# A graph-attention and expert kernel on one core: the last two graphs' router sums taken by columns of row 0, their attention sums put into the products' banks, and the stored lower rows read as they lie

## The chip, the cores and the metric

The kernel runs on one core of a Trainium2 chip. A core has TensorE (PE, the matrix engine; the loads of its stationary operand are shown apart, as PEld), VectorE (DVE), ScalarE (ACT), GpSimd (POOL) and SyncE (SP, which here only issues transfers), an on-chip memory of 128 partitions, and eight accumulator banks of 128 x 512 f32 that only PE writes. The metric is the time on the device, in microseconds (us), median of several runs.

## What is computed

`x` holds 128 graphs of 128 nodes with 1024 features, `adj` one 128 x 128 matrix of zeros and ones for each. For every graph:

```python
x = x + gnn(layernorm(x), adj)      # Wh = x W; one attention weight for each source node and head
x = x + ffn(layernorm(x))           # ffn(y) = y + sum over 2 of 8 experts: up_e (down_e y) * gate_e
```

The gates of a graph come from row 0 of its normalized features alone: eight logits (row 0 times the router's eight rows), the two largest, and a softmax over them. `down` takes 1024 features to 16 for each expert (128 lower rows for all eight), `up` takes them back.

## The kernel before

Graphs are taken in pairs (q = 0 to 63), and pairs in groups of four graphs. A pair's projection `x W` is done with fewer products than the plain block scheme (seven per pair, of which some are shared with the neighbouring pair: the lines 561 and 640). Its result, split in a high and a low part (`parts`, made by `high` on ACT, L708, and by `low` on DVE, L712), is multiplied by the adjacency matrix (`attend`, L770); the attention weight, ELU and residual follow on DVE and ACT, then the second layer norm's sums, the transposed copy `y_t` that the experts read, the logits, the choice, and the expert products.

The order of the work is written out by hand: FIRST, EVEN, ODD and LAST are lists of short names. A name stands for a closure in a table (`does`), and each engine's instructions stand in the order in which the names call for them. Nothing reorders them: an instruction that waits holds up everything behind it on its engine. LAST is the list of the last step. A trailing `-` or `+` means the step before or the one after; the names with `+` come from `at_the_end()`, which treats the last group by itself:

- Set A is graphs 0 and 1 of that group, set C its graphs 2 and 3 (the last two of all; r = 0 and 1). Unlike all groups before, whose chosen experts' rows are fetched one slot at a time, these take all 128 lower rows and all 128 upper rows. `LW` (`load_all`) loads them over the weights that are no longer needed: `up_all`, and `down_of_rows`, in which a partition holds, for each of the 128 lower rows, eight consecutive values (k = 0 to 7, the eight blocks of 128 features).
- `OA` (`order_all`, L1037) copies `down_of_rows` on ACT so that for each k the 128 lower rows' values lie side by side (`down_all`).
- `dA`, `d0C`, `d1C` (`down_of`, L1210) are the lower products: for each k one matmul with 128 x 128 of `down_all` as the stationary operand, over 256 columns of `y_t` for set A (both graphs at once), over 128 columns for each graph of C.
- `A`, `w`, `E`, `a`, `b` + r + h: the attention sum of graph r, half h (L1054), its weighting into `sums_of` (L1060), the exponential (L1068), and the two parts of ELU added to `x` (L1072, L1079). `T` and `k`: transposing a half on PE (L1106) and copying it into `y_t` (L1109). `n`, `q`, `s`: the mean, the squares (L1088), the statistics on POOL.
- `PA`, `P0`, `P10`, `P11`: row 0 times the router's rows, elementwise (L1128, L1135); `R` sums, `L` and `V` (L1151, L1156) add over the partitions on PE; `ch`, `sp`, `rt`, `wg` choose and make the gates, `g` (L1219) multiplies the lower products by them. For set C row 0 is read from the transposed `x`, so the logits of C come after `T`.
- `u` + t + h + set (`up_of`, L1224): the upper product of one graph and half. `m` and `v`: its scaling on ACT (L1237) and its sum with `x` on POOL (L1247), or both at once on DVE (`add_of_up`, L1230). `m..B`, `v..B` finish the group before in the same way. Each half of `x` is stored as soon as it is complete.

Banks: `pw0` and `pw1` (two banks each) hold projections, `ph`, `pl`, `pd_all`, `pu` take turns in two more pairs (`double`, `single`). A name that needs a bank waits until its last reader is done.

Of the kernel before, what the change touches and what calls it, by code (L numbers as in the profile page):

```python
# [8 lines left out]
F32 = mybir.dt.float32  # L9
# [5 lines left out]
ALU = mybir.AluOpType  # L15
# [31 lines left out]
LAST = """  # L47
Jt2- n0- hi0- lo0- J7- J1- q0- ps3- Jt3- Jp- y1- ro1- Jr- I1- n1- t0- J2- Jd- sr- q1- ps2-
J5- It0- J4- st1- Ja- Js- st0- M7b- J3- It1- M7a- Ip- rj0- Je- rp- c22- I6- ss- L- It2- ch0-
hi3- I7- t1- ch1- It3- fr- M4a- fe4- M4b- jn1- Ir- fe0- c21- lo3- hi2- fe5- Ia- I4- ra- rs-  # L50
fe2- I5- fe1- I2- fe7- Is- I3- lo2- A1 Ie- fe6- Id- hi1- fe3- aw M1b lo1- M1a jn0- pe LW+
aw2 fe8- p1 A0 h1 M2a x1 M2b h0 rj1- x0 e1 eo y1 hi0 sc0 e0 lo0 y0 M6b M6a wg n1 q1 D t0 u2
u4 f n0 hi1 dn aw0+ lo1 M7a M7b LR+ q0 pe0+ c22 U0 M4b ss t1 hi3 M4a dw0+ v00 rj0 v01 rdA+
U1 m1B+ lo3 v1B+ m0B+ c21 aw1+ rj1 A00+ pe1+ hi2 A01+ w00+ w01+ v0B+ A11+ a01+ dw1+ a00+
E01+ jn1 b01+ m2B+ PA+ w11+ lo2 RA+ E00+ T01+ A10+ m3B+ b00+ w10+ n0+ LA+ OA+ a11+ a10+ q0+
s0+ E11+ VA+ T00+ dA+ E10+ chA+ k00+ b10+ spA+ b11+ k01+ T10+ T11+ n1+ v3B+ rtA+ wgA+ P11+
k11+ P10+ gA+ u00A+ q1+ P0+ m00A+ RC+ v2B+ LC+ u01A+ jn0 s1+ rdC+ chC+ VC+ m01A+ v00A+ v01A+
k10+ d1C+ spC+ rtC+ ac u10A+ d0C+ m10A+ wgC+ gC+ u11A+ j1+ u00C+ m11A+ u10C+ j0+ v10A+ u01C+
v10C+ v00C+ u11C+ v11C+ v01C+ v11A+
""".split()  # L60
# [3 lines left out]
def adj_ffn_kernel(  # L64
# [959 lines left out]
    down_of_rows = block[0][:, D:2 * D].rearrange("p (e r k) -> p e r k", e=E, r=R)  # L1024
    down_all = block[1][:, 0:D].rearrange("p (k e r) -> p k e r", e=E, r=R)
    router_all = block[1][:, D:D + E * KC]

# [5 lines left out]
    def load_router():  # L1033
        nc.sync.dma_start(router_all, router_table)

    def order_all():
        nc.scalar.copy(down_all, down_of_rows.rearrange("p e r k -> p k e r"))  # L1037

    def at_the_end():
# [10 lines left out]
        def attend_half(r, h):  # L1050
            if i + r not in PH:
                PH[i + r] = double("ph")
            for s in range(2):
                nc.tensor.matmul(PH[i + r][:, h], GRP[g]["adj_f"][:, 2 + r, :],  # L1054
                                 PARTS[p][:, s, NH * r + h], start=(s == 0), stop=(s == 1))
# [44 lines left out]
        def turn_half(r, h):  # L1100
            if h not in turned:
                turned[h] = slot_of(h)
            pt = turned[h][:, r].rearrange("p (c n) -> p c n", c=CPH)
            for c in range(CPH):
                k = h * CPH + c
                nc.tensor.transpose(pt[:, c], X[i + r][:, k * P:(k + 1) * P], ident)  # L1106

        def keep_half(r, h):
            nc.scalar.copy(y_of(i + r)[:, h * CPH:(h + 1) * CPH],  # L1109
                           turned[h][:, r].rearrange("p (c n) -> p c n", c=CPH))  # L1110

# [18 lines left out]

        def parts_of_half(r, h):
            k = slice(h * CPH, (h + 1) * CPH)
            part = prod_of("C")[:, r:r + 1, :, k]
            rows = turned[h][:, r].rearrange("p (o c n) -> p o n c", o=1, c=CPH)[:, :, 0:1]
            nc.vector.tensor_tensor(part, rows.to_broadcast(part.shape),  # L1135
                                    router[:, :, :, k].to_broadcast(part.shape), ALU.mult)

# [10 lines left out]
        def logits_of(s):  # L1148
            n = sets[s][1]
            got["pl", s] = double("pl")  # L1150
            nc.tensor.matmul(got["pl", s][:, 0, 0:n * E], ones, add_of(s)[:, 0:n * E], start=True,  # L1151
                             stop=True)

        def dev_of(s):
            n = sets[s][1]
            nc.tensor.matmul(got["pl", s][:, 1, 0:n], ones, add_of(s)[:, n * E:], start=True,  # L1156
                             stop=True)

        def choose_of(s):
            n = sets[s][1]  # L1160
            shape = [P, n, E]
            by_order = order[:, None].to_broadcast(shape)
            lg = got["pl", s][:, 0, 0:n * E].rearrange("p (g e) -> p g e", g=n)
            top = small.tile([P, TOP, n], F32, tag="top", name="top", bufs=2)
            val = got["val", s] = small.tile([P, 2, n, TOP], F32, tag="val", name="val", bufs=2)
            mark = small.tile(shape, F32, tag="mark", name="mark", bufs=2)
            for c in range(TOP):
                if c:
                    left = small.tile(shape, F32, tag="lg", name="lg", bufs=1)
                    nc.vector.tensor_tensor(mark, by_order, val[:, 0, :, 0:1].to_broadcast(shape),  # L1170
                                            ALU.is_equal)
                    nc.vector.scalar_tensor_tensor(left, mark, NO_ENTRY, lg, op0=ALU.mult,
                                                   op1=ALU.add)
                    lg = left
                nc.vector.tensor_reduce(top[:, c], lg, AX.X, ALU.max)
                nc.vector.tensor_tensor(mark, lg, top[:, c, :, None].to_broadcast(shape),
                                        ALU.is_equal)
                nc.vector.tensor_tensor(mark, mark, by_order, ALU.mult)
                nc.vector.tensor_reduce(val[:, 0, :, c], mark, AX.X, ALU.max)
            pr = got["pr", s] = small.tile([P, 2, n], F32, tag="pr", name="pr", bufs=2)  # L1180
            nc.vector.tensor_tensor(pr[:, 0], top[:, 1], top[:, 0], ALU.subtract)

        def spread_of(s):
            pr = got["pr", s]
            nc.vector.tensor_tensor(pr[:, 0], pr[:, 0], got["pl", s][:, 1, 0:sets[s][1]], ALU.mult)

# [5 lines left out]
        def gates_of(s):  # L1192
# [4 lines left out]
            nc.vector.tensor_mul(gate[:, :, 1], pr[:, 1], gate[:, :, 0])  # L1197
            val = val.rearrange("p v g s -> p v (g s)")
            hit = small.tile([P, n * TOP], F32, tag="own", name="hit", bufs=2)
            nc.vector.tensor_scalar(hit, val[:, 0], own_order, None, op0=ALU.is_equal)  # L1200
            nc.vector.tensor_tensor(hit, hit, val[:, 1], ALU.mult)
            gates = got["gate", s] = small.tile([P, n], F32, tag="gate" + s, name="gate_all", bufs=1)
            nc.vector.tensor_reduce(gates, hit.rearrange("p (g s) -> p g s", g=n), AX.X, ALU.add)

        def down_of(s, t, n):
            if ("pd", s) not in got:
                got["pd", s] = double("pd_all")[:, 0]
            first = sets[s][0] + t
            for k in range(KC):
                nc.tensor.matmul(got["pd", s][:, t * P:(t + n) * P],  # L1210
                                 down_all[:, k].rearrange("p e r -> p (e r)"),
                                 st["y_t"][:, k, first * P:(first + n) * P],
                                 start=(k == 0), stop=(k == KC - 1))

        def gate_of(s):
            n = sets[s][1]
            dn = got["dn", s] = work.tile([P, n, P], F32, tag=sets[s][3], name="dn_all", bufs=1)
            pd = got["pd", s][:, 0:n * P].rearrange("p (t n) -> p t n", t=n)
            nc.vector.tensor_tensor(dn, pd, got["gate", s][:, :, None].to_broadcast(pd.shape),  # L1219
# [40 lines left out]
        for t in range(G):  # L1260
            does.update({f"m{t}B": (scale_before, t), f"v{t}B": (add_before, t)})
        for t in range(2):
            for h in range(2):
                does.update({f"m{t}{h}A": (scale_up, "A", t, h)})
        for r in range(2):
# [3 lines left out]
                f"q{r}": (squares_at_end, r), f"s{r}": (stats_at_end, r), f"j{r}": (join, i + r),  # L1269
                f"d{r}C": (down_of, "C", r, 1)})  # L1270
            for h in range(2):
# [3 lines left out]
                    f"b{r}{h}": (below_half, r, h), f"T{r}{h}": (turn_half, r, h),  # L1275
                    f"k{r}{h}": (keep_half, r, h), f"P{r}{h}": (parts_of_half, r, h)})
        for s in sets:
# [4 lines left out]
            for t in range(2):  # L1282
                for h in range(2):
                    does.update({f"u{t}{h}{s}": (up_of, s, t, h), f"v{t}{h}{s}": (add_of_scaled if s == "A" else add_of_up, s, t, h)})
        does.update({"PA": (parts_of, "A", 0, 2, slice(0, KC)), "dA": (down_of, "A", 0, 2),
                     "P0": (parts_of, "C", 0, 1, slice(0, KC)), "LW": (load_all,), "LR": (load_router,),
                     "OA": (order_all,)})
        return does

# [181 lines left out]
```

## Time and profile before

| | us |
|---|---|
| median of three runs (1859.14 to 1860.34) | 1860.15 |
| the profiled execution, its own time | 1858.17 |
| its span, first to last instruction | 1856.3 |
| PE busy in the span | 1839.1 (99%) |
| DVE busy | 1578.4 (85%) |
| ACT busy | 1242.8 (67%) |
| last product of the projection (L561) ends | 1819.08 |
| last matmul ends | 1850.74 |

An engine's busy time is the union of its instructions. PE is pipelined: records of matmuls overlap, an f32 matmul leaves two records and two loads of its stationary operand, and the distance from one start to the next says more than the length of a record. The span ends some 4 us after the last addition, when the last stores have landed and the engines have met.

### The profile page before, as it was taken

To read this page: it belongs to the slowest core of one execution; us is meant where nothing else is said; L and a number is where in the kernel's file an instruction comes from. 1 tells how busy PE (TensorE), PEld (TensorE's weight loads), DVE (VectorE), ACT (ScalarE), POOL (GpSimd) and SP (SyncE) were. 2 spreads that over 40 slices of the span, in tenths; PEclk is the share of its full clock that TensorE was granted. 3 is DMA by queue.
4 is the path that set the end of the run, shared out by engine and by line. 5 is a ranking of instruction groups with operands and counts; after the bars stand their busy time and mean duration, and the time that the engine had idled before them with its cause. 6 is when DMAs were issued, how large, how long until landed. Compare 5 with 4: busy or idle time off the path is not lost.

```text
span 1856.3 us, 29668 instructions
## 1 busy us (share of the span) xinstructions
PE 1839.1 (99%) x10196; PEld 1504.2 (81%) x10196; DVE 1578.4 (85%) x3411; ACT 1242.8 (67%) x1423; POOL 1172.0 (63%) x1691
## 2 busy tenths in 40 slices
PE   9999999999999999999999999999999999999997
PEld 6888888888888888888888888888888888888884
DVE  6888888888888888888888888888888888888886
ACT  3666666766666766666666667666667676666676
POOL 4666656667566667566666566675666675666663
PEclk9999999999999999999999999999999999999998
DMA  8555566565576655666555665555665556665543
GB/s 321 151 175 140 186 199 177 185 180 149 183 197 190 182 152 168 192 184 194 177 138 187 199 177 183 179 150 183 194 194 182 136 184 192 184 193 173 136 160 114
DMA packets 349100, 330.42 MB, mean 178 GB/s; under 512 B 279196, under 2 KB 281372, under 8 KB 348440
## 3 DMA queue, kind: packets, MB, share of 16 engines
q1 hardware_dynamic: 331512, 287.09, 51.0%
q0 software_dynamic: 17008, 40.91, 7.4%
q8 instruction: 81, 1.33, 0.3%
q14 instruction: 67, 0.55, 0.1%
q10 hardware_dynamic: 432, 0.53, 0.1%
HBM read 194.24 MB, written 68.17 MB: 141 GB/s over the span
## 4 chain that ended last, share of the span: by engine, by line
PE 93%; POOL 3%; DVE 2%; issue 1%; ACT 0%; DMA 0%; DVEq 0%; POOLq 0%
PE pw L561 58%; PE pw L640 17%; PE ph L770 6%; PE pu L1006 4%; PE pd L986 3%; PE ix L640 3%; POOL down L971 2%; PE pd_all L1210 0%; POOL xt L493 0%; PE pu L1224 0%; ACT ph L802 0%; DVE w_sb L1293 0%; DVE w_sb L306 0%; POOL s L493 0%; PE idle L238 0%
## 5 line engine op out<-in xcount | busy, mean ns | idle before, releaser
L561 PE MATMUL pw<-w_sb,xt 128*128 128x260 f32 (+1 forms) x4080 | 959.3, 386 | 0.5 <-POOL w_sb L357 0.5
L561 PEld LDWEIGHTS pw<-w_sb,xt 128*128 128x128 f32 x4080 | 763.1, 190 | 169.2 <-issue 30.6
L971 POOL DMA_INDIRECT down<-table,at_down x248 | 249.3, 1005 | 197.2 <-DVE of_slot L935 116.1
L708 ACT ACTIVATE parts<-wh,rstd 128x512 fp32r<-128x512 f32 x192 | 135.2, 720 | 344.1 <-DVE wh L568 303.7
L849 ACT COPY y_t<-tt 128x2048 uint16<-128x2048 uint16 x126 | 314.6, 2497 | 1.3 <-DMA tt<-halves 1.3
L561 PE MATMUL pw<-w_sb,s 128*128 128x260 f32 (+1 forms) x1088 | 249.8, 382 | 0.0
L843 ACT COPY halves<-xn 128x2048 uint16<-128x2048 uint16 x126 | 237.5, 1885 | 2.5 <-DVE xn L793 2.0
L561 PEld LDWEIGHTS pw<-w_sb,s 128*128 128x128 f32 x1088 | 206.4, 190 | 34.1 <-DVE wh L568 0.9
L493 POOL TENSOR_TENSOR s<-xt 128x512 f32<-128x512 f32 x64 | 83.3, 1302 | 234.6 <-DMA xt<-in_x_t 234.6
L786 ACT ACTIVATE ph<-ph 128x1024 f32<-128x1024 f32 x126 | 127.9, 1015 | 80.4 <-DVE xn L783 73.6
L1015 DVE SCALAR_TENSOR_TENSOR xn<-pu,rstd,xn 128x512 f32<-128x512 f32 x244 | 168.7, 743 | 11.1 <-PE pu L1006 11.1
L776 DVE TENSOR_TENSOR ph<-ph,att 128x1024 f32<-128x1024 f32 x126 | 149.1, 1228 | 11.1 <-PE ph L770 4.5
L432 DVE BATCH_NORM_STATS2 stats<-xn 128x6 f32<-128x512 f32 x248 | 158.4, 680 | 0.0
L855 ACT ACTIVATE xn<-xn,off,mul 128x1024 f32<-128x1024 f32 x128 | 157.6, 1232 | 0.1
L793 DVE SCALAR_TENSOR_TENSOR xn<-ph,xn 128x1024 f32<-128x1024 f32 x126 | 153.2, 1216 | 0.2
L783 DVE SCALAR_TENSOR_TENSOR xn<-ph,xn 128x1024 f32<-128x1024 f32 x126 | 147.9, 1213 | 0.1
L802 ACT ACTIVATE ph<-xn,acc 128x1024 f32<-128x1024 f32 x126 | 140.9, 1119 | 9.0 <-POOL acc L798 8.7
L712 DVE SCALAR_TENSOR_TENSOR parts<-wh,rstd,parts 128x512 fp32r<-128x512 f32 x192 | 140.3, 744 | 4.2 <-ACT parts L708 0.5
L770 PE MATMUL ph<-parts,adj_f 128*128 128x512 f32 x504 | 142.1, 423 | 0.0
L640 PE MATMUL pw<-w_in,s 128*128 128x260 f32 x496 | 129.3, 383 | 0.0
L640 PE MATMUL pw<-w_sb,i 128*128 128x260 f32 x496 | 129.2, 383 | 0.0
L770 PEld LDWEIGHTS ph<-parts,adj_f 128*128 128x128 f32 x504 | 92.7, 188 | 24.2 <-issue 6.2
(235 smaller groups left out, 2676.1 us busy)
## 6 DMA issues: line engine op xcount, KB each, us to landing
xn<-in_x SPq DMA_DIRECT2D x128, 512.0 KB
xt<-in_x_t SPq DMA_DIRECT2D x127, 512.0 KB
out_y<-xn SPq DMA_DIRECT2D x124, 512.0 KB
adj_f<-in_adj_t POOLq DMA_DIRECT2D x32, 256.0 KB
adj_i<-in_adj SPq DMA_DIRECT2D x32, 256.0 KB
down<-table,at_down POOLq DMA_INDIRECT x248
w_sb<-in_w SPq DMA_DIRECT2D x3, 1040.0 KB
wt_sb<-in_w_t SPq DMA_DIRECT2D x1, 2048.0 KB
```

The costliest lines, as they stand in the source:

```text
L432: nc.vector.bn_stats(st[:, h, :], X[i][:, h * HALF:(h + 1) * HALF])
L561: nc.tensor.matmul(banks[name][:, j, cols], lhs()[:, k, :], w_sb[:, rhs, k, j, cols], start=(fresh and k == 0), stop=(k == KH - 1), skip_g ...
L640: nc.tensor.matmul(bank(name), sums(lhs)[:, k], w_of[rhs][:, k], start=(fresh and k == 0), stop=(k == KI - 1), skip_group_check=not fresh)
L770: nc.tensor.matmul(PH[i][:, h], GRP[g]["adj_f"][:, t, :], PARTS[q][:, s, NH * (i % 2) + h], start=(s == 0), stop=(s == 1))
L776: nc.vector.tensor_tensor(ph, ph, ATT[i // 2, None][:, i % 2, :, None].to_broadcast([P, H, F]), ALU.mult)
L783: nc.vector.scalar_tensor_tensor(X[i], whole(i), 0.0, X[i], op0=ALU.max, op1=ALU.add)
L793: nc.vector.scalar_tensor_tensor(X[i], whole(i), 1.0, X[i], op0=ALU.min, op1=ALU.add, accum_out=acc[:, 0:1])
L843: nc.scalar.copy(halves, X[i].bitcast(U16).rearrange("p (d s) -> p s d", s=2))
L849: nc.scalar.copy(y_of(i).bitcast(U16).rearrange("p k (n s) -> p s k n", s=2), TT.pop(i).rearrange("p (s k) n -> p s k n", s=2))
L855: nc.scalar.activation(X[i], X[i], AF.Identity, bias=GRP[g]["off"][:, t:t + 1], scale=GRP[g]["mul"][:, t:t + 1])
L971: nc.gpsimd.indirect_dma_start(out=st["down"][:, j * R:(j + 1) * R].rearrange("p r k -> p (r k)"), out_offset=None, in_=table, in_offset=b ...
L1015: nc.vector.scalar_tensor_tensor(y[:, cols], st["pu", h][t], st["rstd"][:, t:t + 1], y[:, cols], op0=ALU.mult, op1=ALU.add)
```

## The change

Only the last step changes: the list LAST, and closures of `at_the_end`.

1. **Lower rows as they lie.** `OA` and `down_all` go. `down_of` takes its stationary operand from `down_of_rows`, where the 128 values of one k stand eight elements (32 bytes) apart. Set A's product of both graphs becomes two of one graph each (`d0A`, `d1A`).
2. **Row 0 of set C by columns.** `P0`, `P10`, `P11` go. `LX` (`load_rows`) fetches row 0 of the two graphs' input from `x_t`, 128 x 8 single elements each. `xc` (`row_columns`) works out the attention sum of row 0 alone: for each of eight blocks and two parts, a matmul with 128 x 128 of `parts` as the stationary operand over the first two columns of the adjacency matrix, and two matmuls (64 columns wide) that spread the attention weights of row 0, which `xw` has masked. `xs`, `xe`, `xa`, `xb` make ELU and residual of it on small tiles, `PC` multiplies by the router.
3. **Banks.** The attention sums of r go into one of the projection's own banks (`slot_of(r)`), as do the transposes of r. The lower product, the logits and the deviations of a set share one tile (`banks_of`).
4. **Smaller ones.** The comparison `hit` moves from `wg` into `ch`. Graph 1 of set A is added on DVE rather than scaled on ACT and added on POOL.
5. **The order.** LAST is written anew: the attention of r = 0 (`A00` to `b01`) now stands ahead of the last product's result (`c21`) and of the group before's additions, `xc` stands behind the lower products of A, the upper products of A between the halves of `T`, and so on.

```diff
-U1 m1B+ lo3 v1B+ m0B+ c21 aw1+ rj1 A00+ pe1+ hi2 A01+ w00+ w01+ v0B+ A11+ a01+ dw1+ a00+
-E01+ jn1 b01+ m2B+ PA+ w11+ lo2 RA+ E00+ T01+ A10+ m3B+ b00+ w10+ n0+ LA+ OA+ a11+ a10+ q0+
-s0+ E11+ VA+ T00+ dA+ E10+ chA+ k00+ b10+ spA+ b11+ k01+ T10+ T11+ n1+ v3B+ rtA+ wgA+ P11+
-k11+ P10+ gA+ u00A+ q1+ P0+ m00A+ RC+ v2B+ LC+ u01A+ jn0 s1+ rdC+ chC+ VC+ m01A+ v00A+ v01A+
-k10+ d1C+ spC+ rtC+ ac u10A+ d0C+ m10A+ wgC+ gC+ u11A+ j1+ u00C+ m11A+ u10C+ j0+ v10A+ u01C+
-v10C+ v00C+ u11C+ v11C+ v01C+ v11A+
+M7a y1 t1 u4 LR+ u2 f D hi1 aw0+ n1 pe0+ lo1 dw0+ c22 A00+ q1 dn A01+ M4b w01+ w00+ U0 ss
+a01+ rj0 a00+ M4a E00+ hi3 b00+ v00 E01+ lo3 b01+ v01 c21 U1 rj1 T00+ T01+ aw1+ rdA+ PA+
+m1B+ hi2 pe1+ lo2 xw0+ k00+ A10+ n0+ m0B+ k01+ A11+ dw1+ v1B+ RA+ v0B+ d0A+ w10+ w11+ LA+
+m2B+ xw1+ m3B+ jn0 E11+ a11+ VA+ E10+ q0+ a10+ d1A+ chA+ spA+ b11+ xc1+ rtA+ wgA+ xc0+ xs+
+T11+ xe+ s0+ gA+ xa+ u00A+ b10+ n1+ jn1 xb+ PC+ j0+ T10+ RC+ k10+ u10A+ LC+ q1+ chC+ u11A+
+v2B+ u01A+ s1+ k11+ v10A+ d0C+ rdC+ VC+ v3B+ spC+ ac m01A+ rtC+ wgC+ m00A+ d1C+ gC+ j1+
+u10C+ u11C+ v00A+ v11A+ v10C+ u00C+ u01C+ v00C+ v11C+ v01A+ v01C+
...
-    def order_all():
-        nc.scalar.copy(down_all, down_of_rows.rearrange("p e r k -> p k e r"))
...
-                PH[i + r] = double("ph")
+                PH[i + r] = slot_of(r)
...
+        def load_rows():
+            got["row"] = work.tile([P, 2, KC], F32, tag="s4", name="row_x", bufs=2)
+            for r in range(2):
+                nc.sync.dma_start(got["row"][:, r], x_t[i + r, :, :, 0])
...
+            for k in range(KC):
+                h, c = divmod(k, CPH)
+                for s in range(2):
+                    nc.tensor.matmul(sums[:, 2 * k:2 * k + 2],
+                                     PARTS[p][:, s, NH * r + h, c * P:(c + 1) * P],
+                                     GRP[g]["adj_f"][:, 2 + r, 0:2], start=(s == 0), stop=(s == 1))
+            of_f = got["row_att"][:, r].rearrange("p (k f) -> p f k", f=2)
+            for f in range(2):
+                nc.tensor.matmul(atts[f * F:(f + 1) * F, 0:KC], ones[:, 0:F], of_f[:, f], start=True,
+                                 stop=True, tile_position=(0, f * F))
...
         def down_of(s, t, n):
-            if ("pd", s) not in got:
-                got["pd", s] = double("pd_all")[:, 0]
             first = sets[s][0] + t
             for k in range(KC):
-                nc.tensor.matmul(got["pd", s][:, t * P:(t + n) * P],
-                                 down_all[:, k].rearrange("p e r -> p (e r)"),
+                nc.tensor.matmul(banks_of(s)[:, 0, t * P:(t + n) * P],
+                                 down_of_rows.rearrange("p e r k -> p (e r) k")[:, :, k],
                                  st["y_t"][:, k, first * P:(first + n) * P],
                                  start=(k == 0), stop=(k == KC - 1))
```

## The prediction

> **What bounds the kernel now.** I read the page first. PE is busy for 99% of the span, so up to the last projection nothing but PE's own work counts, and the change leaves that work as it is. What can move is the end, and its view is PE's timeline from the last projection on (start, length, operation, how many records, in brackets the idle time before and what ended it):
>
> ```profile
> 1815.30 3.77 PE L561 MATMUL pw<-w_sb,xt 128*128 128x260 f32 x16
> 1819.01 1.14 PE L1006 MATMUL pu<-up,dn 32*128 32x512 f32 x8
> 1821.50 1.20 PE L1054 MATMUL ph<-parts,adj_f 128*128 128x512 f32 x4 [1.35 <-ACT part_up L1237]
> 1824.17 0.70 PE L1054 MATMUL ph<-parts,adj_f 128*128 128x512 f32 x2 [1.47 <-DVE sums_of L1060]
> 1826.82 1.12 PE L1106 MATMUL pw<-ident,xn 128*128 128x128 f32 x4 [1.95 <-DVE xn L1079]
> ...
> 1830.56 4.67 PE L1210 MATMUL pd_all<-y_t,w_sb 128*128 128x256 f32 x16
> 1835.06 1.04 PE L1106 MATMUL pw<-ident,xn 128*128 128x128 f32 x8
> ...
> 1841.76 2.02 PE L1210 MATMUL pd_all<-y_t,w_sb 128*128 128x128 f32 x16 [1.22 <-DVE pr L1185]
> ...
> 1844.48 1.95 PE L1210 MATMUL pd_all<-y_t,w_sb 128*128 128x128 f32 x16
> 1846.27 4.46 PE L1224 MATMUL pu<-w_sb,dn_all 128*128 128x512 f32 x10
> ```
>
> From 1820.16, where L1006 ends in the chain, to 1850.74 PE has 30.6 us, of which the brackets of the whole view add up to 7.4 us of waiting. The rest is work, and the chain of waits agrees: L1210 and L1224 lead it in this window with 22.3% and 17.0%. Part of the work ran at half clock, as the windows view shows (PE busy, PEclk granted, DMA):
>
> ```profile
> 1822.43:1825.84 3.41, 0.97 (x4) 1.00 0.76 308
> 1825.84:1829.26 3.42, 2.44 (x9) 0.50 0.00 0
> 1829.26:1832.67 3.41, 3.41 (x12) 0.50 0.00 0
> 1832.67:1836.08 3.41, 3.41 (x20) 1.00 0.00 0
> ```
>
> The third view, one line's instructions, decides the forecast. L986, the lower products of all groups before, reads its stationary operand as the changed L1210 will, eight elements apart, but 32 columns at a time; L367 loads 32 columns that lie side by side. L287 has both kinds as the moving operand (`down_sb` strided, 128 columns). Durations in ns, shortest, median, longest:
>
> ```profile
> L986 PEld LDWEIGHTS pd<-y_t,down x1984: 135/138/173, 117.1 to 1810.2; 128*32 128x32 f32 x199
> L986 PE MATMUL pd<-y_t,down x1984: 272/273/330, 117.1 to 1810.3; 128*32 128x128 f32 x199
> ```
> ```profile
> L367 PEld LDWEIGHTS ps<-xt,a_two x16: 106/110/110, 40.5 to 41.0; 128*32 128x32 f32 x16
> ```
> ```profile
> L287 PE MATMUL pc<-down_sb,mean_of x16: 396/412/416, 72.6 to 73.3; 128*32 128x128 f32 x16
> ```
>
> A side-by-side load takes 110 ns for 32 columns and 190 for 128 (L561's row), so 0.83 ns a column over some 83. The strided load of 32 takes 138: (138 - 83) / 32 = 1.72 ns a column, twice as much. The moving side says the same: 128 columns take 273 side by side and 412 strided, 139 more, where 128 columns cost 107. And ACT's `OA`, the very copy that goes, needs 2102 ns for 1024 elements 32 bytes apart, where L1109 copies 512 in 580.
>
> **The change part by part.** The profiled execution took 1858.17, 2.0 below the median of 1860.15; I add differences of its trace to the median.
>
> *Strided stationary operand.* L1210 over 128 columns is paced at 1.98 / 16, less the last record's tail, 0.112 us a record: load (107) and stream (107) overlap. With a load of 128 x 1.72 = 220 ns the load sets the pace: 0.23 a record, the distance at which L287's strided rounds come (four tiles a round, four rounds in 1.12 less the tail). Bounds: 0.112 if the load were as fast as before, 0.33 if load and stream no longer overlapped. I take 0.23, from the same stride. Products are now 64 records, 14.7 us; before they were 16 at 0.216 and 32 at 0.112, 7.0 at full clock. So 7.7 more, on PE, with PE never idle around them: all of it on the path.
>
> *Columns of row 0.* 32 matmuls over two columns are paced by their loads, 0.108 apart side by side; with eight records of half-width loads 3.9 us (bounds 3.5, nothing for those eight; 4.9, at the 0.13 between L1156's records). They stand on PE ahead of `T10`, the upper products of A and everything of C. What they buy is that C's logits no longer wait for the second half of graph 3; before, that wait and the choice after it are PE's 0.24 and 1.22.
>
> *`OA` out.* 2.10 of ACT, from 1827.76 on; `q0`, `E10`, `E11` come earlier. PE's products wait for it before; now they are not paced by it. Worth what PE's waits are worth, below.
>
> *The order.* `w`, `a`, `b` of r = 0, six DVE operations of 0.61 to 0.69 (L1060, L1072, L1079), now stand before `c21`. Its read ended at 1819.8 and goes to some 1823.7. Behind it on DVE: five small ones (0.9), `PA` (0.37), `lo2` (0.74). So the attention of r = 1 runs through from 1825.9; before, its last part came at 1827.80 to 1829.16. PE's idle time of 1.47 and 1.95 shrinks to about 1.9 before `U1`'s second half and 0.7 before `A10`, for PE now also has `U1` and eight transposes there.
>
> *Transfers.* `LX` goes onto SP's queue behind `LW`, near 1802, ahead of both DMA transposes. Two issues, 0.4 to 0.6 each by L1029 and L1031. The first transpose is issued at 1810.2 and its reader on ACT starts at 1816; the rows are needed at about 1839. 37 us cover 2048 elements on 16 engines up to 0.29 us an element. Nothing, unless they stop the queue. Row-sum operations on DVE (five of about 0.2) take the place of L1135 and the 0.84 of L1128. `hit` earlier, graph 1 on DVE: about nothing, except that three additions instead of two now stand behind the last matmul, 0.67 more.
>
> *Sum, full clock.* From 1825.9: three attends 0.7, products of A 7.4, logits and deviations 0.4, columns 3.9: 1838.3. Row sums and gate multiply on DVE 0.9 (transposes beside it): 1839.2. Four upper products 3.44 (L1224, 0.86 each), transposes 0.44, logits of C 0.2: 1843.3. First products of C 3.7, deviations 0.2, wait for `sp` 0.25, second 3.7: 1851.2. Gate multiply 0.5, four upper products 3.44, tail 0.2: 1855.3. Three additions 2.1: 1857.4. Before, the last addition ended at 1852.17. Difference +5.2.
>
> *Clock.* In the trace a stretch of 3.41 us with PE busy for 28% is followed by half clock; 1839.50 to 1842.91, 57% busy, is not. After the change the stretch to 1825.84 has half of L1006 (1.1), eight transposes (0.9) and one attend (0.3), near 50%; and the columns leave 3.9 us in which hardly anything streams. I count one stretch at half clock, 3.41 / 2 = 1.7; bounds 0 and 5.1 (three). Sum +6.9: 1867.0.
>
> Two rules of the Trainium skill, which the sums don't need. "SBUF — State Buffer", section "Door 1: The DMA port swizzle", says that reads which cross into a new 16-byte line each time pay a penalty, so f32 may be strided by four for free; eight is beyond that, and the rows above agree. "TensorE: Matmul & The Clock Gate", section "LDWEIGHTS (loading the stationary operand)", prices a load by its columns alone, columns / 1.2 ns, whatever their stride: 107 for 128, which would put the time at about 1858; L986 against L367 speaks against it.
>
> **The rivals.** *Loads at full rate* (the other side: not slower). If a full-width strided load hid behind the stream, the sum loses 64 x 0.118 = 7.6: 5.2 - 7.6 = -2.4, so 1857.8, or 1859.5 with one slow stretch. For it: L986's rounds of four tiles still come every 0.11. Against: each of those loads has only 32 columns, and 32 x 1.72 = 55 fits under the stream; 220 doesn't. It decides below some 0.15 a record. *Half clock for two or three stretches*: 5.2 + 3.4 or 5.1, 1868.8 to 1870.5. For it: products paced by loads stream for 107 of 230 ns, 46%, between the two values above. Against: the loads may count as work, which no row shows. *No overlap of load and stream* (0.33): 6.4 more, 1873; against it, L1210's 0.112. *Row transfers late or stopping the queue*: 3 to 10 more; against it, the 37 us.
>
> **How the numbers follow.** Strided loads with one slow stretch (1867.0) 0.32; with none (1865.3) 0.25; with two or three 0.25; full rate 0.13; no overlap or late transfers 0.05. 0.2% is 3.7 us, about what a measurement of this kernel can tell from no change: above 1863.9 slower, below 1856.4 faster. Slower holds the slow cases less a little of the one with no slow stretch, 0.81; same 0.16, mostly the full-rate rival; faster 0.03. The range leaves out that rival and the last one: 1862 to 1871.
>
> **What would show it.** Right: L1210's successor with 64 records about 0.23 apart and loads near 300 ns; columns as 32 records 0.11 apart; no copy of 2.10 on ACT; PE without a gap over 1 us from 1826 on; last matmul near 1855 to 1857. Wrong: loads of 190 ns and products 0.11 apart; a wait of DVE for `row`; half clock over more than two stretches. The least certain step is the pace of full-width strided loads, which no row shows directly.

## The result and the profile after

The changed kernel takes 1872.21 us, median of six runs (1870.17 to 1874.24); the kernel before, in the same comparison, 1860.24 (1859.14 to 1862.52). The ratio is 1.0063, 95% interval 1.005 to 1.0076: 12.0 us slower, where 6.9 were forecast and 1862 to 1871 was the range. (The ratio is worked out over all runs, so it can differ a little from the quotient of the two medians.) The profiled execution took 1871.61, with a span of 1869.8; its last addition ends at 1865.50, before at 1852.17.

PE's timeline after the change (start, length, operation, records; in brackets the idle time before and what ended it):

```profile
1791.45 0.41 PE L899 MATMUL pl<-add,ones 128*128 128x36 f32 x2 [1.30 <-POOL add L877]
...
1798.67 3.77 PE L561 MATMUL pw<-w_sb,xt 128*128 128x260 f32 x16 [0.59 <-DVE wh L665]
...
1820.63 2.02 PE L561 MATMUL pw<-w_sb,xt 128*128 128x260 f32 x8
1822.59 1.13 PE L1006 MATMUL pu<-up,dn 32*128 32x512 f32 x4
1825.18 2.08 PE L1006 MATMUL pu<-up,dn 32*128 32x512 f32 x4 [1.47 <-DVE xn L1015]
1827.18 1.97 PE L1102 MATMUL pw<-ident,xn 128*128 128x128 f32 x8
1828.80 2.06 PE L1050 MATMUL pw<-parts,adj_f 128*128 128x512 f32 x4
1830.66 3.88 PE L1254 MATMUL banks<-y_t,w_sb 128*128 128x128 f32 x16
...
1838.57 1.93 PE L1150 MATMUL cols<-adj_f,parts 128*128 128x2 f32 x16
...
1843.99 2.04 PE L1268 MATMUL pu<-w_sb,dn_all 128*128 128x512 f32 x2
...
1850.65 3.84 PE L1254 MATMUL pw<-y_t,w_sb 128*128 128x128 f32 x16
...
1854.96 4.16 PE L1254 MATMUL pw<-y_t,w_sb 128*128 128x128 f32 x16 [0.34 <-DVE pr L1233]
1859.72 3.67 PE L1268 MATMUL pu<-w_sb,dn_all 128*128 128x512 f32 x8 [0.61 <-DVE dn_all L1263]
```

The first two lines stand before the last projection ends: PE waits there, which it did not before. The two identical L1006 halves take 1.13 and 2.08 us, and one upper product (L1268, two records) 2.04 where four take 3.67: part of this stretch ran at half clock. From 1825.18 on PE waits nowhere for more than 0.61.

The windows view (stretch, its length, PE busy, number of records, PEclk, DMA), cut to the clock's own grid of 3.41 us:

```profile
1821.75:1825.16 3.41, 1.96 (x9) 1.00 0.00 0
1825.16:1828.58 3.42, 3.40 (x11) 0.50 0.38 153
1828.58:1831.99 3.41, 3.41 (x13) 0.50 0.00 0
...
1835.40:1838.82 3.42, 3.42 (x18) 1.00 0.00 0
1838.82:1842.23 3.41, 3.41 (x34) 1.00 0.00 0
1842.23:1845.64 3.41, 3.41 (x14) 0.50 0.00 0
1845.64:1849.06 3.42, 3.42 (x10) 0.50 0.38 153
...
1855.88:1859.30 3.42, 3.24 (x14) 0.50 0.20 77
```

Five stretches ran at half clock, 17 us of the last 41, against two before. Behind the first gap (1.96 of 3.41 us busy) there are two, and two more behind 1838.82 to 1842.23, in which PE is busy throughout by its records; these are the columns of row 0. The fifth lies under set C's second product and costs next to nothing: that product takes 4.16 us, and 4.07 in an execution without the slow stretch (the run below with three more matmuls).

The strided loads, in the view of one line (shortest, median, longest in ns):

```profile
L1254 PEld LDWEIGHTS banks<-y_t,w_sb x32: 313/337/342, 1830.4 to 1838.3; 128*128 128x128 f32 x32
L1150 PEld LDWEIGHTS cols<-adj_f,parts x32: 186/192/337, 1838.5 to 1842.4; 128*128 128x128 f32 x32
```

A load of 128 columns 32 bytes apart takes 337 ns, one side by side 192 at full clock. Sixteen products take 3.7 to 4.2 us in the chain of waits, 0.23 us a record, as forecast.

Where the profiled execution stands against the forecast, stretch by stretch (the forecast's sum at full clock, without its 1.7 us for the clock):

| stretch | forecast | measured | more |
|---|---|---|---|
| up to set A's first product starts | 1826.6 | 1830.66 | 4.1 |
| products of A, columns | 11.7 | 12.4 | 0.7 |
| from the columns' end to C's first product | 5.0 | 7.6 | 2.6 |
| from there to the last matmul | 12.0 | 12.7 | 0.7 |

Of the 4.1, 0.6 was there long before the last step's order begins to differ (the L561 at 1758.76 before starts at 1759.39 after; in other executions of the changed list it starts anywhere from 1758.59 to 1759.95, so this is spread), and 1.9 is PE's idle time from 1788.30 to 1801.95.

What the slow clock cost can be read against runs below. From the last half of the projection (L561, 1820.63) to set A's first product it is 10.03 us here and 7.96 in two runs with the same work there whose clock stayed full: 2.1 us. From the start of the columns to set C's first product it is 12.08 us, and 9.75 in the run whose columns stream 256 wide and keep the clock full: 2.3 us. Together that is 4.4 us, more than the 1.9 of idle time.

### The profile page after: what moved, and what is told of

Same layout as the page of the kernel before. It is cut to its first block, busy times and chain, and to the rows that moved or that the text cites. A ratio compares the mean times of both kernels' runs of the same rounds, so it can differ in the third digit from the quotient of the medians.

```text
span 1869.8 us, 29775 instructions
## 1 busy us (share of the span) xinstructions
PE 1854.3 (99%) x10252; PEld 1518.9 (81%) x10252; DVE 1580.9 (85%) x3417; ACT 1240.4 (66%) x1421; POOL 1168.4 (62%) x1689
## 5 line engine op out<-in xcount | busy, mean ns | idle before, releaser
L561 PE MATMUL pw<-w_sb,xt 128*128 128x260 f32 (+1 forms) x4080 | 959.3, 386 | 1.2 <-DVE wh L665 0.6
L561 PEld LDWEIGHTS pw<-w_sb,xt 128*128 128x128 f32 x4080 | 762.8, 190 | 169.9 <-issue 31.2
L561 PE MATMUL pw<-w_sb,s 128*128 128x260 f32 (+1 forms) x1088 | 249.8, 382 | 0.0
L561 PEld LDWEIGHTS pw<-w_sb,s 128*128 128x128 f32 x1088 | 206.4, 190 | 34.1 <-DVE wh L568 0.9
L786 ACT ACTIVATE ph<-ph 128x1024 f32<-128x1024 f32 x126 | 127.8, 1015 | 83.3 <-DVE xn L783 79.5
L776 DVE TENSOR_TENSOR ph<-ph,att 128x1024 f32<-128x1024 f32 x126 | 149.1, 1228 | 11.8 <-PE ph L770 5.7
L802 ACT ACTIVATE ph<-xn,acc 128x1024 f32<-128x1024 f32 x126 | 140.9, 1118 | 8.8 <-POOL acc L798 8.6
```

What stands on the lines that cost most here:

```text
L561: nc.tensor.matmul(banks[name][:, j, cols], lhs()[:, k, :], w_sb[:, rhs, k, j, cols], start=(fresh and k == 0), stop=(k == KH - 1), skip_g ...
L776: nc.vector.tensor_tensor(ph, ph, ATT[i // 2, None][:, i % 2, :, None].to_broadcast([P, H, F]), ALU.mult)
```

## Experiments

All times are medians. Runs came in three groups, each with its own runs of the kernel before: 1859.61 for the first four, 1859.32 for the next four, 1858.91 for the last three. The changed kernel itself was run only in the comparison above, so each difference is taken to the kernel before of its own group.

**Loads side by side.** The changed kernel, reading other values.

```diff
-                                 down_of_rows.rearrange("p e r k -> p (e r) k")[:, :, k],
+                                 down_lying[:, k],
...
+    down_lying = block[0][:, D:2 * D].rearrange("p (k c) -> p k c", k=KC)
```

> The changed kernel, but each lower product loads 128 neighbouring values of the stored rows instead of 128 values 32 bytes apart (other values, so the lower products are not the reference's; the amount of work is the same). Theory (strided loads pace the products at 0.23 us a record): L1254's successor shows loads near 190 ns and records 0.11 apart, the 64 records take 7 us instead of 14.7, and the time falls by 5 to 7.6 us, to 1864.6 to 1867.2; the lower end of the gain if gates are then waited for. Rival (the products are slow for another reason, such as the clock or the banks): records stay 0.2 apart or more, time within 1 us of 1872.2.

1862.90 us, ratio 1.0017 (1.0008 to 1.0026): 3.3 above its kernel before instead of 12.0, and below the range expected. The loads:

```profile
L1255 PEld LDWEIGHTS pw<-y_t,w_sb x32: 186/192/192, 1844.5 to 1848.9; 128*128 128x128 f32 x32
```

Set C's two products of 16 records take 1.95 and 2.02 us instead of 3.84 and 4.16. So the rival falls, and 8.7 of the 12.0 us go with the stride, somewhat over the 64 x 0.118 = 7.6 worked out from the pace. Not all of the 8.7 need be the loads themselves: this profile shows three stretches at half clock instead of five. The run with the rows stored by k, further down, gives the loads alone.

**Columns streamed 256 wide.** The result of each column stands in the range that the next matmul overwrites, so the sums of row 0 are not the reference's here; the work is.

```diff
-                    nc.tensor.matmul(sums[:, 2 * k:2 * k + 2],
+                    nc.tensor.matmul(sums[:, 2 * k:2 * k + 2 * P],
...
-                                     GRP[g]["adj_f"][:, 2 + r, 0:2], start=(s == 0), stop=(s == 1))
+                                     both, start=(s == 0), stop=(s == 1))
...
+            both = GRP[g]["adj_f"][:, 1 + r:3 + r].rearrange("p g n -> p (g n)")
```

> The changed kernel, but each matmul of the columns of row 0 streams 256 columns (both graphs' adjacency) instead of 2; the number of matmuls and of loads is the same, and the unused columns are written over. Theory (matmuls over two columns load but hardly stream, so the clock gate takes PE for idle and halves the clock for two stretches of 3.41 us after them): columns still 4 to 5 us, but transposes and upper products behind them at full clock (0.86 instead of 1.7 us each), time 2 to 3.2 us less, 1869 to 1870.2. Rival (something else cools the clock, such as the products paced by loads ahead of the columns): half clock in the same place, time 0 to 1 us more.

1868.35 us, ratio 1.0045 (1.0031 to 1.0059): 8.7 above its kernel before, 3.2 less than the change, a little more of a gain than expected. The columns take 4.6 us from the first record to what follows them, against 4.5, and behind them the clock stays (windows view, same columns):

```profile
1838.82:1842.23 3.41, 3.13 (x24) 1.00 0.00 0
1842.23:1845.64 3.41, 3.41 (x14) 1.00 0.24 97
```

Streaming 128 times as many columns made the kernel faster. The profiles of all runs with columns say the same. Between the start of the columns and set C's first product, the four with columns two wide (after, loads side by side, squares moved back, three more matmuls) have one to three stretches at half clock; the six with columns 256 wide have none. So at this place it is the streaming that counts, not how long PE is taken up.

The rival, that products paced by strided loads cool the clock, falls for this place with the profile after: 1835.40 to 1838.82 holds hardly anything else, and the clock stays full behind it. It does not fall everywhere. A stretch at half clock lies under set C's second product, behind strided products and a wait of 0.34 us, in four of the five profiles that have strided loads and the new list, and in none of the five with side-by-side loads. The strided loads hardly notice it there (4.16 against 4.07 us).

In the profile with wide columns the first two slow stretches are missing too, although nothing was changed there: the grid lies elsewhere, and the stretch that holds most of the gap is 2.09 us busy (1823.11 to 1826.53) instead of 1.96. The same work between the same two lines takes 7.96 us instead of 10.03:

```profile
1819.90 2.02 PE L561 MATMUL pw<-w_sb,xt 128*128 128x260 f32 x8
...
1827.86 4.10 PE L1256 MATMUL banks<-y_t,w_sb 128*128 128x128 f32 x16
```

So part of the 3.2 us may come from executions like this one. By the traces the columns' own share differs from execution to execution: from their start to set C's first product the four profiles with columns two wide take 10.41, 12.07, 12.08 and 13.67 us, against 9.75 here.

**The squares moved back.**

```diff
-t1- st0- sr- ps2- J4- Js- M7b- Ja- Ip- J3- t0- Je- q1- M7a- st1- I2- ss- I6- rs- jn0- rp-
+t1- q1- st0- sr- ps2- J4- Js- M7b- Ja- Ip- J3- t0- Je- M7a- st1- I2- ss- I6- rs- jn0- rp-
```

> The changed kernel, with one name moved in the last step's list: the squares of the second graph of the pair before (q1-) ahead of the copies for the transposes, as in the list before the change, instead of behind an ACT copy that waits for a POOL addition. Theory (the new head of the list delays PE's logits at 1791.45 by 1.30 us, and all behind them): that wait goes, PE's last projection ends 1.3 to 1.9 us earlier, and so does the end: 1870.3 to 1870.9. Rival (the wait is only taken over by the choice on DVE or by a later wait of PE): PE's idle time moves, time within 0.5 us of 1872.2.

1870.48 us, ratio 1.0056 (1.0042 to 1.007): 10.9 above its kernel before, 1.1 less than the change; 1.3 to 1.9 less was expected, and the two intervals overlap, so the median alone does not settle it. The trace does: the wait of 1.30 is gone, the one of 0.59 behind it stays, and from the L561 near 1759 to the last one PE takes 59.8 us instead of 61.2:

```profile
1789.91 0.31 PE L899 MATMUL pl<-add,ones 128*128 128x36 f32 x2
...
1797.14 3.77 PE L561 MATMUL pw<-w_sb,xt 128*128 128x260 f32 x16 [0.59 <-DVE wh L665]
```

The chain can be read on two queues of the changed kernel. ACT's copy waits for POOL, and the squares (L802) stand behind it and a second copy; POOL's addition L649, in turn, stands behind four others (1782.40 to 1785.85), before behind one:

```profile
1786.58 0.38 ACT L646 COPY ip<-ix 128x260 f32<-128x260 f32 x1 [4.74 <-POOL u L649]
1786.85 1.90 ACT L843 COPY halves<-xn 128x2048 uint16<-128x2048 uint16 x1
1788.65 1.12 ACT L802 ACTIVATE ph<-xn,acc 128x1024 f32<-128x1024 f32 x1
```

**The rows alone.** The kernel before with part 1 only.

```diff
-                                 down_all[:, k].rearrange("p e r -> p (e r)"),
+                                 down_of_rows.rearrange("p e r k -> p (e r) k")[:, :, k],
...
-E01+ jn1 b01+ m2B+ PA+ w11+ lo2 RA+ E00+ T01+ A10+ m3B+ b00+ w10+ n0+ LA+ OA+ a11+ a10+ q0+
+E01+ jn1 b01+ m2B+ PA+ w11+ lo2 RA+ E00+ T01+ A10+ m3B+ b00+ w10+ n0+ LA+ a11+ a10+ q0+
```

> The kernel before with one part of the change alone: the lower products read the stored rows as they lie, and the copy OA is left out. Theory (0.23 us a record whatever else is there): set A's 16 records of 256 columns keep their 0.22 to 0.29, set C's 32 records go from 0.112 to 0.23 apart, 3.8 us more, of which the missing copy gives back up to 1: 1863 to 1864.3. Rival (strided loads hide as before): C's records stay 0.11 apart, time 1859 to 1860.5.

1863.66 us, ratio 1.0021 (1.0012 to 1.003), 4.05 more, as expected. Its L1206 takes 4.77 us for set A's 16 records of 256 columns (4.67 before, both with about their first 2 us at half clock) and 4.16 and 3.87 for C's (2.02 and 1.95 before). With 256 columns behind each load the stride is nearly free; with 128 it is 0.12 us a record. That the change also splits A's 16 records into 32 is what makes the price about double.

**Three more matmuls in the first gap.**

```diff
-a01+ rj0 a00+ M4a E00+ hi3 b00+ v00 E01+ lo3 b01+ v01 c21 U1 rj1 T00+ T01+ aw1+ rdA+ PA+
+a01+ rj0 a00+ M4a E00+ hi3 b00+ v00 E01+ lo3 b01+ v01 c21 WB+ U1 rj1 T00+ T01+ aw1+ rdA+ PA+
...
+        def keep_warm(n):
+            turned[0] = slot_of(0)
+            for _ in range(n):
+                nc.tensor.matmul(turned[0][:, 0, 0:2 * P], ident, up_all[:, 0:2 * P], start=True,
+                                 stop=True)
```

> The changed kernel with three more matmuls (256 columns each, 1.3 us together) into a free bank ahead of the second half of the group before's upper products, where PE sits idle for 1.47 us. Theory (where the clock's grid of 3.41 us falls so that the stretch with this gap counts as idle, the clock is halved behind it, at the cost of 2.7 us; it fell so in one profile of two): the stretch behind is at full clock in every profile, median 0.5 to 2.5 us less, 1869.7 to 1871.7. Rival (the gap never matters, or DVE is what is waited for at full clock too): within 0.5 us of 1872.2, or slower by up to 0.5 where the extra work delays the upper products.

1870.72 us, ratio 1.0063 (1.0049 to 1.0077), 11.4 more than its kernel before: 0.6 less than the change, which cannot be told from none. The clock behind the gap is full in its profile, but PE then waits there:

```profile
1829.17 0.97 PE L1050 MATMUL pw<-parts,adj_f 128*128 128x512 f32 x3 [1.06 <-DVE parts L712]
```

At full clock DVE's `lo2` is late instead, so part of what the slow clock costs here was hidden. The median does not decide between theory and rival; the traces show both at work. From the last half of the projection to set A's first product it is 8.79 us here, 10.03 and 9.78 in the two executions of the same list with slow stretches there, and 7.96 in the two without. The extra matmuls save 1.0 to 1.2 us where the grid falls badly and cost 0.8 where it does not.

**Head, columns and gap together.** The list up to `LW` as before the change, the columns 256 wide with the same graph's adjacency twice, and the three matmuls.

```diff
+            twice = GRP[g]["adj_f"][:, 2 + r:3 + r].to_broadcast([P, 2, P])
...
-                                     GRP[g]["adj_f"][:, 2 + r, 0:2], start=(s == 0), stop=(s == 1))
+                                     twice, start=(s == 0), stop=(s == 1))
```

> The changed kernel with the head of the list as it was before the change (all names up to LW), the columns of row 0 streamed 256 wide (the adjacency of the same graph twice, so that the sums stay the reference's), and the three matmuls of the run before it. The strided loads stay. Theory (the time over the forecast came from PE's waits at the head, 1.9 us, and from half clock): the parts add up, 1.9 and 3.3 and 0.5 to 2, so 1865 to 1866.5, what the forecast without any half clock gave (1865.3). Rival (the parts overlap: DVE's and ACT's work is waited for as soon as PE is earlier): 1867 to 1869.

1866.55 us, ratio 1.004 (1.0026 to 1.0054), 7.2 more than its kernel before: the parts nearly add up, just above what was expected. All five runs lie between 1866.37 and 1866.85, where the change spreads over 4 us.

**The copy back, on POOL.**

```diff
+    def order_all():
+        nc.gpsimd.tensor_copy(down_all, down_of_rows.rearrange("p e r k -> p k e r"))
...
-E00+ hi3 b00+ v00 E01+ lo3 b01+ v01 c21 WB+ U1 rj1 T00+ T01+ aw1+ rdA+ PA+ m1B+ hi2 pe1+ lo2 xw0+
+E00+ hi3 b00+ v00 E01+ lo3 b01+ v01 c21 WB+ U1 rj1 T00+ T01+ aw1+ rdA+ OA+ PA+ m1B+ hi2 pe1+ lo2 xw0+
```

> The run before it, and the copy of the lower rows back, on POOL instead of ACT, where POOL is idle from 1819 to 1824; the products load neighbouring values again. Theory (strided loads cost 8 us): 1857 to 1858.5, below the kernel before by 1 to 3 us. Rival (POOL's copy of 1024 elements 32 bytes apart takes longer than its 5 us and slows DVE beside it, or the gates are waited for): 1859 to 1862.

1861.66 us, ratio 1.0007 (0.9998 to 1.0016). The copy takes 2.05 us, and DVE's two additions beside it 3.13 instead of 1.28 in the run without it:

```profile
1817.36 2.05 POOL L1037 COPY w_sb<-w_sb 128x1024 f32<-128x1024 f32 x1
```
```profile
1817.43 3.13 DVE L1072 SCALAR_TENSOR_TENSOR xn<-sums_of,xn 128x512 f32<-128x512 f32 x2
```

PE waits 1.47 us inside `U1` again, which the run without the copy does not, and a stretch at half clock is back behind it. The rival holds, by its second half: the copy itself is short, but it slows DVE beside it. Without the extra matmuls:

> The run before it without the three extra matmuls. Theory (they only pay where the grid falls so that their gap counts as idle): 0.5 to 2 us more than that run, and half clock in some profiles. Rival (they do nothing): the same time within 0.5 us.

1861.38 us, ratio 1.0012 (1.0003 to 1.0021): the same within what can be told, so the extra matmuls do nothing for the median here.

**The kernel before with its gaps filled.**

```diff
-U1 m1B+ lo3 v1B+ m0B+ c21 aw1+ rj1 A00+ pe1+ hi2 A01+ w00+ w01+ v0B+ A11+ a01+ dw1+ a00+
+U1 m1B+ lo3 v1B+ m0B+ c21 aw1+ rj1 A00+ pe1+ hi2 A01+ WB3+ w00+ w01+ v0B+ A11+ WB4+ a01+ dw1+ a00+
```

> The kernel before with seven more matmuls (256 columns each) into a free bank in PE's two gaps of 1.47 and 1.95 us near 1823 and 1826, three and four of them. Theory (the spread between runs of one kernel, 1858.0 to 1863.7 for the kernel before, is where the clock's grid of 3.41 us falls on these gaps): the stretches behind the gaps are at full clock in every run, the runs lie within 1 us of each other, and the median falls by 0.5 to 2 us, to 1857.5 to 1859. Rival (the spread has another cause, or the gaps' own waits set the time): spread and median as before, or 0.3 us more where the extra work is in the way.

1858.62 us, ratio 0.9995 (0.9986 to 1.0004), runs from 1856.5 to 1860.67. The theory falls: it asked for runs within 1 us of each other, and the spread stays at 4 us; the median cannot be told from the kernel before, though four of the eleven runs lie below the fastest of the 27 beside them. In its profile set A's products run at full clock (3.72 us instead of 4.67), but a slow stretch appears later, on C's first product, which takes 3.66 where the second takes 1.95:

```profile
1840.46 3.66 PE L1217 MATMUL pd_all<-y_t,w_sb 128*128 128x128 f32 x16 [0.46 <-ACT y_t L1116]
...
1844.83 1.95 PE L1217 MATMUL pd_all<-y_t,w_sb 128*128 128x128 f32 x16
```

Two gaps were filled, and four more follow between 1835 and 1841. What the whole spread of the kernel before comes from stays open.

**Rows stored by k.** A second table is written early, with the values ordered by k, and the last step loads that one.

```diff
+        nc.scalar.copy(by_k[0][:, k], down_sb.rearrange("p e r k -> p k (e r)")[:, k])
...
+            nc.sync.dma_start(table_all, by_k[0].rearrange("p k c -> p (k c)"))
...
+        nc.sync.dma_start(down_all.rearrange("p k c -> p (k c)"), table_all)
```

> The run with the old head, wide columns and three extra matmuls (1866.55), but the lower rows are stored a second time early in the kernel, ordered by k (four copies of 256 elements on ACT in the second step), and the last step loads that table, so that the products' loads are side by side and no copy is needed in the last step. Theory (strided loads cost 64 x 0.118 us and nothing waits otherwise): 1858 to 1859.5, equal to or up to 1.5 us below the kernel before. Rival (gates or DVE's additions are waited for as soon as the products are short): 1860 to 1862.

1861.36 us, ratio 1.001 (1.0001 to 1.0019). The tail did what the theory says: from the first lower product to the last matmul 22.4 us (1830.62 to 1853.05), against 30.4 with strided loads in the run that it is built on (1827.81 to 1858.21), where the rest of the last step is the same: 8.0 us for the stride. But that product starts 2.8 us later in the span; 1.1 of it is a wait in the second step, among the four copies that were put on ACT there, and the run that it is built on has no such wait:

```profile
88.18 1.14 PE L651 MATMUL pw<-w_sb,s 128*128 128x260 f32 x4 [1.09 <-DVE parts L723]
```

That the copies cause it, and where the other 1.7 comes from, was not tried; neither theory named that place. With `PA` behind `lo2` on DVE:

> The run before it, with the elementwise product of set A's row 0 (PA) behind the low part lo2 on DVE instead of ahead of it. Theory (PE waits 1.1 us for lo2 before A10): lo2 0.37 us earlier, the time 0.2 to 0.4 us less than the run before it. Rival (something else is waited for at that place): the same within 0.2.

1861.54 us, ratio 1.001 (1.0001 to 1.0019). PE's wait for `lo2` shrinks from 1.07 to 0.82, and nothing of it can be seen in the median. No version tried here beats the kernel before by more than the noise.

## Why the prediction was right in its direction and short in its size

- **Strided stationary operand: right.** 0.23 a record was taken, 0.23 was measured, with loads of 337 ns (near 300 was forecast). The 7.7 us on the path are 8.0 when only the loads' order differs in the tail (30.4 against 22.4), and 8.7 by the run with side-by-side loads, in which fewer slow stretches help. The rules of the Trainium skill that were weighed come out as the rows had them: "SBUF — State Buffer", section "Door 1: The DMA port swizzle", is right that a stride of eight f32 is not free; columns / 1.2 ns, in "TensorE: Matmul & The Clock Gate", section "LDWEIGHTS (loading the stationary operand)", gives an estimate of 107 ns for both kinds, where the pace measured is 112 for the one and 232 for the other.
- **"The change leaves that work as it is": the first step that failed.** The forecast started at the last projection and took PE's work ahead of it as unchanged. The new list moves `q1-` on ACT behind a copy that waits for POOL, and PE idles for 1.9 us between 1788 and 1802, where the forecast had nothing. Moving the one name back removes 1.3 of it in the trace and returned 1.1 in the median. The trace of before shows the risk: there the squares L802 stand ahead of that copy L646.
- **Clock: the step that failed by most; mechanism right, size wrong.** One stretch (1.7 us) was taken, with up to three as a bound. There were five in the profiled execution, the sign of being wrong that the prediction had named, and the traces put them at 4.4 us, not 1.7: 2.1 at the first gap, 2.3 at the columns, next to nothing at the fifth. The forecast had named both places and then counted one stretch for the two together. For the first gap it weighed that 57% busy had passed at 1839.50; here 57% did not pass, and in two other executions of the same code 61% and 62% did (2.09 and 2.12 us). So the busy share of one trace could not carry that choice; where the grid falls was luck, and what exactly the clock counts stays open. The rival with two or three stretches named the right term, but gave it to the products paced by loads. A stretch full of them kept the clock full, and the slow stretch that does follow them cost about 0.1 us.
- **Columns: 3.9 taken, 4.5 measured** (4.3 in the run with side-by-side loads, where the clock was full under nearly all of them): within the bounds given.
- **Order: right.** `c21` was read from 1825.04 to 1825.73; the forecast's 1823.7 with the 0.6 of offset and the 1.9 of the head is 1826.2. PE's idle time before the second half of `U1` was forecast at 1.9 and is 1.47.
- **Transfers: right.** Each issue of `LX` took 0.7 to 0.9 instead of 0.4 to 0.6, and nobody waited for them.
- **Not foreseen, and free:** the choice of set A now waits until its product is done: DVE idles for 5.33 us and is released by L1254, though the logits (L1195) were done at 1834.66. Logits and product now share one tile; that this is the reason was not tried. The columns cover it. (The opening says that only PE writes the accumulator banks. The traces show others: DVE's L776 and ACT's L786 read `ph` and write it in place.)

## What to carry to other kernels

Before a transposing copy is dropped, look at how many columns stream behind each strided load: with 256 the stride was nearly free here, with 128 it cost 0.12 us a record. When a hand-written order is replaced, compare every queue from its first differing name, not only from the edit that is meant; one moved name on ACT cost PE 1.3 us thirty microseconds ahead of the place that the change is about. Where short matmuls mostly load, as the columns here did, look at the granted clock behind them, however busy PE looks. And compare clocks over several executions: a stretch at half clock that one profile shows another may not.

## What was not expected of the hardware

- Strided loads do not notice the clock. In the profile after, L1254's loads take 337 ns at half clock (1830.4 to 1831.9) and 337 at full clock. Side-by-side loads do: the columns' loads in the run with the squares moved back, in the slow stretch from 1837.4 on, take 333 instead of 192. At half clock the two kinds cost the same:

```profile
L1150 PEld LDWEIGHTS cols<-adj_f,parts x16: 288/333/338, 1837.4 to 1840.5; 128*128 128x128 f32 x16
```

- Where the clock's grid falls differs from one execution to the next: the same code at the first gap was followed by two slow stretches in the profile after and in the run with side-by-side loads, and by none in two others. "TensorE: Matmul & The Clock Gate", section "What's actually happening", calls the window free-running, and these profiles agree.
- A copy on POOL from and to SBUF held up DVE's additions with two SBUF inputs by 1.85 us (3.13 against 1.28). "SBUF — State Buffer", section "SBUF: two separate sides", says that such an addition and a POOL operation that reads SBUF exclude each other for the whole instruction, whichever starts first; this run agrees, with the copy (2.05 us) starting 0.07 us ahead.
